# A convolution, attention and mixture-of-experts kernel: parts of the second convolution on ScalarE and GpSimd, fewer small copies, and VectorE's bursts cut into parts

## The chip, the cores and the metric

The kernel runs on one core of a Trainium2 chip. The core has TensorE (PE, matrix products), VectorE (DVE), ScalarE (ACT) and GpSimd (POOL), and SyncE (SP), whose queue here issues most DMAs. Each engine takes its own instructions in the order in which they stand in its queue. The metric is the device time of one launch in microseconds; a median over several launches is given.

## The reference

The input is 8 images of 56 x 56 positions with 256 channels, in float32. Two layers follow.

```python
# layer 0: 32 paths p, each 256 -> 4 -> 4 -> 256 channels, with batch norms
h = relu(bn1(x @ W1[p] + B1[p]))             # 1x1, to 4 channels
h = relu(bn2(conv3x3(h, W2[p]) + B2[p]))     # 3x3, 4 to 4 channels
h = relu(bn3(h @ W3[p] + B3[p]))             # 1x1, back to 256 channels
x = relu(sum_over_paths(h) + x)
# layer 1, on tokens t = x as (8, 3136, 256)
y = layernorm(t)
k = v = layernorm per head of 32 channels(y)       # std with n - 1
t = t + (y @ (k^T v / N) per head + y)
z = layernorm(t)
t = t + z + sum over the two best of 8 experts of weight * (gelu(z @ w1[e]) @ w2[e] + b2[e])
```

Each token goes to the two experts with the largest router logits; their weights are the two softmax values scaled to a sum of one.

## The kernel before

The 25,088 tokens are cut into 56 chunks of 448 (8 image rows), seven to an image. A chunk passes through a software pipeline of slots. In slot s the kernel does the third convolution of chunk s (`conv3_steps`), the first of chunk s+2 (`conv1_steps`), the second of chunk s+1 (`conv2_steps`), the head statistics of chunk s-1 (`end_steps`), the attention of chunk s-8 (`attn_steps`), the routing of one or two chunks whose attention is done (`route_steps`), and some tiles of the experts (`moe_steps`). After the 56th chunk's slot come slots with attention, routing and experts alone, and at the end experts alone; this is called the tail.

The order of work on PE, ACT and DVE is written out by hand (`tc.manual_schedule`, line 74). Each list of steps has a stretch of the slot (its low and high end as fractions) and each step a cost; `issue` (L1368) puts every step at the middle of its share of the stretch and issues all of a slot's steps in the order of these positions. Costs thus set places only. POOL and SP are not among the engines ordered by hand: the framework's planner places their instructions.

The parts that the change and the prediction's steps touch:

- Third convolution. For each of 32 steps of a chunk, `pair` (L577) makes two products c (L587); ACT turns the first into r (L592), and DVE adds the second to r (L595). Each product has a PSUM bank of seven (`ps_mm`); r has seven buffers. `sum_paths` (L601) sums four r at a time on PE (su, L608), a unit; there are eight units in a chunk. The sum of unit u stands after the pairs of the unit that follows have begun. After the fourth and the eighth unit DVE makes u (L615).
- Second convolution. After the three rows of taps (L297) ACT writes h2 (L306). The step `halves` (L309) splits it on DVE into hi (L314, rounded) and lo (L315, the rest), which sixteen DMAs on SP (L320) spread into hl, the operand of the next slot's third convolution.
- Head statistics. `means` (L665, a reduction of t and a scaling, both DVE), `center` (L679, POOL), `squares` (L687, ACT), `variances` (L695, eight DVE operations and then the square root as a power on POOL, L719), `inverse` (L723, DVE, which needs that power), `scale` (L735, POOL) and `products` (L742, PE).
- Attention. `attend` (L866) for four quarters: a product, an addition on DVE (L874), the copy of the router's part lg on ACT (L878, put off by one quarter), and token statistics on DVE (L881, L882); after the last the power rs2 on POOL (L885). `means` (L887) then makes nm on DVE, `normed` (L893) the normalised tokens in the payload pay on ACT, and `base` (L899) adds them to X on POOL and stores X.
- Routing. `logit`, `best` twice, `weights`, `ranks` and `rows` (L938 to L1028), nearly all DVE. `rows` writes into a token's payload row its two weights (L1019, L1020) and its number (L1021, from the constant ids) and the place of its row. `scatter` (L1030) then sends the rows by indirect DMAs on POOL into the regions of the experts.
- Experts. `take_rows` (L1220) and `take_weights` (L1231) load a tile of 256 rows (tile z, tag rows, four buffers) and its expert's weights w (four buffers) on SP. `tile_in` (L1239) turns the rows on PE, copies them on ACT (L1249), and copies the rows' weights g (L1252) and numbers index (L1256) on DVE. `tile_mid` (L1279) and `tile_out` (L1295) make the two layers; ACT scales by g into y (L1311); `tile_add` (L1316) adds y into the output by an indirect DMA on POOL (L1325).
- Setup. L487 to L494 split the second bias b2 into two halves, with buffers in the pool of constants, which lives through the kernel.

## Time and profile before

| | us |
|---|---|
| median of 3 runs (lowest, highest) | 3382.8 (3377.44, 3388.03) |
| the profiled execution | 3376.6 |
| its span, first to last instruction | 3374.9 |
| PE busy / DVE busy | 3001.6 / 2179.8 |
| ACT busy / POOL busy | 1895.8 / 1928.4 |
| mean granted PE clock | 0.951 of full speed |

How the views are read. The page's first part has an engine's busy time, its share of the span and its number of instructions (PEld is the loading of weights on PE). The busy time by stretch has, for each stretch of the span, its length and then PE, PEld, DVE, ACT and POOL (with instruction counts), the granted PE clock, the share of DMA busy time and GB/s. A tile's view gives the shortest, median and longest duration of each operation on it in ns, and below who waited for it, in us and times. A line of the order in time has the start and the length in us, engine, line, operation, output and inputs, shape and count, and in brackets how long the engine stood idle before it and what ended that.

### The profile page before, as it was taken

The numbers are of one execution on the slowest core, as the hardware profiler recorded it, in microseconds if no ns is written. First come the engines' busy times: TensorE is split into PE (matmuls) and PEld (weight loads), VectorE is DVE, ScalarE is ACT, GpSimd is POOL, SyncE is SP. The second block draws the span as 40 slices with busy tenths as digits, with TensorE's granted clock in tenths as the row PEclk, the third lists the DMA queues.
The fourth block names the chain that finished last, engine by engine and source line by source line (L and its number), as shares of the span: only waits on it lengthen the run. The fifth ranks groups of instructions, "written<-read, shape, count | busy, mean of one in ns | idle before, by whom it ended". The sixth has DMA issues, their size and how long they took to land. (4 is left out here: it accounts for less than half of the span.)

```text
span 3374.9 us, 55166 instructions
## 1 busy us (share of the span) xinstructions
PE 3001.6 (89%) x16677; PEld 1697.5 (50%) x16677; DVE 2179.8 (65%) x5762; ACT 1895.8 (56%) x3799; POOL 1928.4 (57%) x1386
## 2 busy tenths in 40 slices
PE   5888888888898999999999999899989987888698
PEld 2343433443444554555545555455444545676577
DVE  3666777777877777776776777776777774333200
ACT  2656555545565666566655666566656654443345
POOL 2222244444556566657565666746656657777677
PEclk7999989989999999999999999999999999988799
DMA  6432334445466676666666667567665756888797
GB/s 146 121 86 84 91 103 123 120 123 150 129 162 159 164 197 168 166 165 174 175 163 163 159 185 187 148 177 187 158 180 152 187 149 159 201 217 218 173 222 178
DMA packets 341481, 537.72 MB, mean 159 GB/s; under 512 B 59952, under 2 KB 251584, under 8 KB 341184
## 3 DMA queue, kind: packets, MB, share of 16 engines
q1 hardware_dynamic: 257088, 429.93, 43.8%
q0 software_dynamic: 81984, 103.45, 16.9%
q8 instruction: 134, 2.20, 0.3%
q14 instruction: 163, 1.34, 0.1%
q10 hardware_dynamic: 2112, 0.81, 0.1%
HBM read 248.01 MB, written 192.55 MB: 131 GB/s over the span
## 5 line engine op out<-in xcount | busy, mean ns | idle before, releaser
L595 DVE SCALAR_TENSOR_TENSOR r<-c,nb,r 128x448 f32<-128x448 f32 x1792 | 1127.3, 676 | 556.7 <-ACT r L592 482.8
L592 ACT ACTIVATE r<-c,b3t 128x448 f32<-128x448 f32 x1792 | 1033.2, 636 | 359.4 <-PE c L587 338.6
L1325 POOL DMA_INDIRECT out_dram<-y,index x420 | 662.8, 1578 | 356.3 <-ACT y L1311 243.7
L587 PE MATMUL c<-hl,W3hl 64*128 64x448 f32 x3584 | 708.4, 428 | 74.4 <-ACT r L592 37.7
L608 PE MATMUL su<-r,gather 128*32 128x448 f32 x3584 | 574.5, 568 | 64.9 <-DVE r L595 38.4
L1031 POOL DMA_INDIRECT regions<-pay,rrowi x448 | 433.1, 967 | 314.1 <-PE c L587 204.2
L587 PEld LDWEIGHTS c<-hl,W3hl 64*128 64x128 f32 x3584 | 341.9, 188 | 505.6 <-issue 227.1
L1287 PE MATMUL ph<-eT,w 128*128 128x256 f32 x1680 | 468.1, 410 | 55.7 <-DMA w<-Wd 23.8
L1307 PE MATMUL py<-w,hT 128*128 128x256 f32 x1680 | 435.6, 384 | 0.0
L1311 ACT ACTIVATE y<-py,g 128x256 f32<-128x256 f32 x420 | 196.7, 475 | 402.1 <-PE py L1307 303.1
L1287 PEld LDWEIGHTS ph<-eT,w 128*128 128x128 f32 x1680 | 306.9, 198 | 196.9 <-issue 101.8
L719 POOL TENSOR_TENSOR hsd<-hsd,half 112x36 f32<-112x36 f32 x56 | 351.7, 6280 | 78.4 <-DVE hsd L718 77.7
L1291 ACT ACTIVATE hT<-ph,w 128x256 f32<-128x256 f32 x420 | 198.1, 477 | 308.5 <-PE ph L1287 165.6
L1307 PEld LDWEIGHTS py<-w,hT 128*128 128x128 f32 x1680 | 293.9, 193 | 28.7
L681 POOL TENSOR_TENSOR norm<-t,hmean 112x512 f32<-112x512 f32 x112 | 120.2, 1130 | 322.1 <-PE c L587 175.0
L870 PE MATMUL at<-tab,tT 128*112 128x272 f32 x896 | 266.1, 421 | 11.9 <-ACT y L1311 6.8
L608 PEld LDWEIGHTS su<-r,gather 128*32 128x32 f32 x3584 | 104.2, 110 | 272.9 <-issue 135.5
L1303 PE MATMUL py<-b2hl,own 128*128 128x256 f32 x420 | 178.7, 425 | 22.4 <-ACT pay L894 8.1
L870 PEld LDWEIGHTS at<-tab,tT 128*112 128x112 f32 x896 | 149.4, 181 | 92.0 <-issue 17.3
L297 PE MATMUL c<-R,W2t 96*32 96x448 f32 x1344 | 180.1, 567 | 3.9 <-DMA R<-h 3.0
L894 ACT ACTIVATE pay<-X,nm,rs 112x256 f32<-112x256 f32 x224 | 134.9, 603 | 75.1 <-DVE nm L889 64.4
L976 POOL TENSOR_TENSOR rq<-ebase,rq 112x8 f32<-112x8 f32 (+1 forms) x32 | 52.9, 1654 | 197.0 <-DVE rq L975 197.0
(246 smaller groups left out, 3198.5 us busy)
## 6 DMA issues: line engine op xcount, KB each, us to landing
w<-Wd SPq DMA_DIRECT2D x210, 513.0 KB
rows<-regions SPq DMA_DIRECT2D x210, 259.0 KB
xi<-in_x_dram SPq DMA_DIRECT2D x56, 448.0 KB
hl<-hi SPq DMA_DIRECT2D x448, 56.0 KB
tTs<-u SPq DMA_DIRECT2D x56, 448.0 KB
ts<-t SPq DMA_DIRECT2D x56, 448.0 KB
tT<-tTs SPq DMA_DIRECT2D x56, 448.0 KB
X<-ts SPq DMA_DIRECT2D x56, 448.0 KB
```

What stands on the lines that cost most here:

```text
L587: product = nc.tensor.matmul(tiles[g][:, :CH], W3hl[rows, ab, cg, :], hl[rows, ab, :], start=True, stop=True)
L592: nc.scalar.activation(r, tiles[0][:, :CH], AF.Relu, bias=b3t[:, cg, 2 * ab : 2 * ab + 1])
L595: nc.vector.scalar_tensor_tensor(r, tiles[1][:, :CH], nb3[:, cg, 2 * ab + 1 : 2 * ab + 2], r, op0=ALU.max, op1=ALU.add,)
L608: nc.tensor.matmul(ps[32 * c4 : 32 * c4 + 32, :CH], gather, unit.pop((s, 4 * u + c4)), start=(ab == 0), stop=(ab == NQ - 1),)
L719: nc.gpsimd.tensor_tensor(sd, sd, half[:T, :].rearrange("q (k h) -> q k h", k=KT), ALU.pow)
L870: nc.tensor.matmul(ps, tT[:, f, k * T : (k + 1) * T], tables_of[b][:, f, :], start=(f == 0), stop=(f == NF - 1),)
L1031: ins = nc.gpsimd.indirect_dma_start(out=regions[n], out_offset=bass.IndirectOffsetOnAxis(ap=v["row_i"][:, (m - group[0]) * KT + k, n : n ...
L1287: nc.tensor.matmul(ps, w[:, f * C + hf * P : f * C + (hf + 1) * P], eT[:, f, :], start=(f == 0), stop=(f == NF - 1),)
L1291: nc.scalar.activation(hT[:, hf, :], ps, AF.Gelu, bias=w[:, 2 * NF * C + hf : 2 * NF * C + hf + 1])
L1307: nc.tensor.matmul(ps, hT[:, f, h * P : (h + 1) * P], w[:, (NF + f) * C : (NF + f + 1) * C], start=False, stop=(f == NF - 1),)
L1311: nc.scalar.activation(y[:, h, :], ps, AF.Identity, scale=g[:, h : h + 1])
L1325: ins = nc.gpsimd.indirect_dma_start(out=out_rows, out_offset=at, in_=y[:, h, :], in_offset=None, compute_op=ALU.add, **partial,).ins
```

## The change

- Second convolution: ACT makes both h2 and hi from the PSUM bank (the same activation twice); lo is made by POOL instead of DVE.
- Head statistics: a helper `in_parts` cuts a step into n parts of equal cost, each running to the next `yield`. `means` becomes three parts (two half reductions, then the scaling, now on ACT), with a cost of 0.8 instead of 0.6; `variances` five, `inverse` two.
- Attention: each quarter becomes two parts; the copy of lg and the token statistics stand in the second. A step `number` writes the tokens' numbers into the payload by an iota on POOL; the following `means` has half its cost.
- Routing: `logit`, `best`, `weights` two parts each, `rows` three. The weights are written straight into the payload, without a copy, and the numbers are no longer written there.
- Experts: g is a view of the row tile z and no copy; z has five buffers.
- Setup: the split of b2 moves ahead, with its two intermediate buffers in the setup pool; ids goes.

```diff
@@ -225,6 +225,19 @@
     nc.gpsimd.memset(h1[:, 1 : HW + 1, 0:1], 0.0)
     nc.gpsimd.memset(h1[:, 1 : HW + 1, HW + 1 : W58], 0.0)
 
+    def in_parts(cost, n, fn):
+
+        run = []
+
+        def part(k):
+            if not run:
+                run.append(fn())
+            for _ in run[0]:
+                if k < n - 1:
+                    return
+
+        return [(cost / n, lambda k=k: part(k)) for k in range(n)]
+
     def is_chunk(s):
         return 0 <= s < S
 
@@ -303,16 +316,16 @@
             if dy == 2:
                 del tapped[s]
                 h2 = split.tile([P, CH], F32, tag="h2", name=f"h2_{s}")
-                nc.scalar.activation(h2, ps[0][:, :CH], AF.Relu, bias=sh2, scale=sc2)
-                h2s[s] = h2
+                hi = split.tile([P, CH], F32R, tag="hi", name=f"hi_{s}")
+                for part in (h2, hi):
+                    nc.scalar.activation(part, ps[0][:, :CH], AF.Relu, bias=sh2, scale=sc2)
+                h2s[s] = (h2, hi)
 
         def halves():
 
-            h2 = h2s[s]
-            hi = split.tile([P, CH], F32R, tag="hi", name=f"hi_{s}")
+            h2, hi = h2s[s]
             lo = split.tile([P, CH], F32R, tag="lo", name=f"lo_{s}")
-            nc.vector.tensor_copy(hi, h2)
-            nc.vector.tensor_tensor(lo, h2, hi.bitcast(F32), ALU.subtract)
+            nc.gpsimd.tensor_tensor(lo, h2, hi.bitcast(F32), ALU.subtract)
             hl = hlp.tile([P, NQ, CH], F32R, tag="hl", name=f"hl_{s}")
             for ab in range(NQ):
                 for v, part in enumerate((hi, lo, hi, lo)):
@@ -415,6 +428,15 @@
         nc.vector.tensor_reduce(
             sumb[:, f, :], sub.rearrange("q a n -> q (a n)"), AX.X, ALU.add
         )
+
+    b2hl = const.tile([P, C], F32R, name="b2hl")
+    b2s = setup.tile([P, C], F32, name="b2s")
+    b2l = setup.tile([E, C], F32R, name="b2l")
+    nc.gpsimd.memset(b2s, 0.0)
+    nc.sync.dma_start(out=b2s[:E], in_=b2)
+    nc.vector.tensor_copy(b2hl, b2s)
+    nc.vector.tensor_tensor(b2l, b2s[:E], b2hl[:E].bitcast(F32), ALU.subtract)
+    nc.sync.dma_start(out=b2hl[E : 2 * E].bitcast(F32), in_=b2l.bitcast(F32))
     setup_pool.__exit__(None, None, None)
 
     spill = ctx.enter_context(
@@ -483,15 +505,6 @@
         tc.dram_tile([E * CAPR, ROW], F32, name=f"regions_{k}") for k in range(2)
     ]
     Wd = tc.dram_tile([E, P, WROW], F32, name="Wd")
-
-    b2hl = const.tile([P, C], F32R, name="b2hl")
-    b2s = const.tile([P, C], F32, name="b2s")
-    b2l = const.tile([E, C], F32R, name="b2l")
-    nc.gpsimd.memset(b2s, 0.0)
-    nc.sync.dma_start(out=b2s[:E], in_=b2)
-    nc.vector.tensor_copy(b2hl, b2s)
-    nc.vector.tensor_tensor(b2l, b2s[:E], b2hl[:E].bitcast(F32), ALU.subtract)
-    nc.sync.dma_start(out=b2hl[E : 2 * E].bitcast(F32), in_=b2l.bitcast(F32))
     pos_i = const.tile([P, 2], I32, name="pos_i")
     pos = const.tile([P, 2], F32, name="pos")
     nc.gpsimd.iota(pos_i, [[P, 2]], base=0, channel_multiplier=1)
@@ -503,8 +516,6 @@
     nc.vector.tensor_copy(row_code, row_i)
     nc.vector.tensor_scalar(row_code, row_code, -1.0, float(E), ALU.mult, ALU.add)
 
-    ids = const.tile([T, KT], I32, name="ids")
-    nc.gpsimd.iota(ids, [[T, KT]], base=0, channel_multiplier=1)
     def tiles_after(n):
 
         return max(0, (CH * n - E * (TR - 1)) // TR)
@@ -664,10 +675,14 @@
 
         def means():
             m = v["m"] = small([T, KT, NH], "hmean")
-            nc.vector.tensor_reduce(
-                m, v["t"].rearrange("q k (h c) -> q (k h) c", c=HC), AX.X, ALU.add
-            )
-            nc.vector.tensor_scalar_mul(m, m, 1.0 / HC)
+            for h in range(2):
+                nc.vector.tensor_reduce(
+                    m[:, 2 * h : 2 * h + 2],
+                    v["t"][:, 2 * h : 2 * h + 2].rearrange("q k (h c) -> q k h c", c=HC),
+                    AX.X, ALU.add,
+                )
+                yield
+            nc.scalar.mul(m, m, 1.0 / HC)
 
         def heads(t):
 
@@ -696,9 +711,13 @@
 
             sd = v["sd"] = small([T, KT, NH + 1], "hsd")
             ss = small([T, KT, NH], "hss")
-            nc.vector.tensor_reduce(
-                ss, v["sq"].rearrange("q k (h c) -> q (k h) c", c=HC), AX.X, ALU.add
-            )
+            for h in range(2):
+                nc.vector.tensor_reduce(
+                    ss[:, 2 * h : 2 * h + 2],
+                    v["sq"][:, 2 * h : 2 * h + 2].rearrange("q k (h c) -> q k h c", c=HC),
+                    AX.X, ALU.add,
+                )
+                yield
             m = v["m"]
             mu = small([T, KT], "hmu")
             dm = small([T, KT, NH], "hdm")
@@ -707,10 +726,12 @@
                 dm, mu[:, :, None].to_broadcast([T, KT, NH]), -1.0 / NH, m,
                 op0=ALU.mult, op1=ALU.add,
             )
+            yield
             nc.vector.tensor_mul(dm, dm, dm)
             nc.vector.scalar_tensor_tensor(
                 dm, dm, float(HC), ss, op0=ALU.mult, op1=ALU.add
             )
+            yield
             nc.vector.tensor_reduce(mu, dm, AX.X, ALU.add)
             nc.vector.tensor_scalar(
                 sd[:, :, NH], mu, 1.0 / C, LN_EPS, ALU.mult, ALU.add
@@ -729,6 +750,7 @@
                 op0=ALU.mult, op1=ALU.add,
             )
             nc.vector.reciprocal(inv, inv)
+            yield
             rs1s[s] = keep.tile([T, KT], F32, tag="rs1", name=f"rs1_{s}")
             nc.vector.reciprocal(rs1s[s], sd[:, :, NH])
 
@@ -755,8 +777,9 @@
                 nc.vector.tensor_add(kvs[b], kvs[b], ps)
 
         return [
-            (0.1, begin), (0.6, lambda: turn(0)), (0.6, lambda: turn(1)), (0.6, means),
-            (1.0, center), (0.6, squares), (1.8, variances), (0.8, inverse), (0.8, scale),
+            (0.1, begin), (0.6, lambda: turn(0)), (0.6, lambda: turn(1)),
+            *in_parts(0.8, 3, means), (1.0, center), (0.6, squares),
+            *in_parts(1.8, 5, variances), *in_parts(0.8, 2, inverse), (0.8, scale),
             (1.9, products),
         ]
 
@@ -861,7 +884,6 @@
         mv = stat.tile([T, KT, 2], F32, tag="mv", name=f"mv_{a}")
         rs2 = keep.tile([T, KT], F32, tag="rs2", name=f"rs2_{a}", bufs=4)
         nm = stat.tile([T, KT], F32, tag="nm", name=f"nm_{a}")
-        late = []
 
         def attend(k):
 
@@ -875,9 +897,8 @@
                 X[:, k, :], ps[:, :C], rs1[:, k : k + 1], X[:, k, :],
                 op0=ALU.mult, op1=ALU.add,
             )
-            late.append(lambda: nc.scalar.copy(lg[:, k, :], ps[:, C:]))
-            if k:
-                late.pop(0)()
+            yield
+            nc.scalar.copy(lg[:, k, :], ps[:, C:])
             nc.vector.bn_stats(st[:, k, :], X[:, k, :])
             nc.vector.bn_aggr(mv[:, k, :], st[:, k, :])
             if k == KT - 1:
@@ -885,9 +906,14 @@
                 nc.gpsimd.tensor_tensor(rs2, rs2, mhalf[:T, :KT], ALU.pow)
 
         def means():
-            late.pop(0)()
             nc.vector.scalar_tensor_tensor(
                 nm, mv[:, :, 0], -1.0, rs2, op0=ALU.mult, op1=ALU.mult
+            )
+
+        def number():
+
+            nc.gpsimd.iota(
+                pay[:, :, C + 2].bitcast(I32), [[T, KT]], base=a * CH, channel_multiplier=1
             )
 
         def normed(k):
@@ -908,8 +934,8 @@
             pays[a] = (pay, lg, rs1, rs2)
 
         return (
-            [(1.0, lambda k=k: attend(k)) for k in range(KT)]
-            + [(0.6, means)]
+            sum((in_parts(1.0, 2, lambda k=k: attend(k)) for k in range(KT)), [])
+            + [(0.3, number), (0.3, means)]
             + [(0.4, lambda k=k: normed(k)) for k in range(KT)]
             + [(0.6, base)]
         )
@@ -944,6 +970,7 @@
                     mine, raw[:, :, :E], rs1[:, :, None].to_broadcast([T, KT, E]), ALU.mult
                 )
                 nc.vector.tensor_add(mine, mine, raw[:, :, E:])
+                yield
 
         dsc = desc[:T, None, :].to_broadcast([T, K, E])
 
@@ -963,6 +990,7 @@
                 )
             nc.vector.tensor_reduce(mx, lg, AX.X, ALU.max)
             nc.vector.tensor_tensor(sel, lg, wide(mx), ALU.is_equal)
+            yield
             nc.vector.tensor_tensor(sel, sel, dsc, ALU.mult)
             nc.vector.tensor_reduce(at, sel, AX.X, ALU.max)
             nc.vector.tensor_tensor(sel, dsc, wide(at), ALU.is_equal)
@@ -974,6 +1002,7 @@
                 mine = q[:, n * KT : (n + 1) * KT]
                 nc.vector.tensor_mul(mine, mine, pays[m][3])
             nc.gpsimd.tensor_tensor(q, ebase[:T, :K], q, ALU.pow)
+            yield
             both = v["both"] = small([2, E], "rboth", BF16)
             nc.vector.tensor_copy(both, v["sel"])
 
@@ -1011,14 +1040,15 @@
         def rows():
             q2 = v["q"]
             q1 = small([], "rq1")
-            nc.vector.tensor_scalar_add(q1, q2, 1.0)
-            nc.vector.reciprocal(q1, q1)
+            nc.vector.scalar_tensor_tensor(
+                q1, q2, 1.0, half[:T, :K], op0=ALU.add, op1=ALU.max
+            )
             for n, m in enumerate(group):
                 pay = pays[m][0]
                 mine = slice(n * KT, (n + 1) * KT)
-                nc.vector.tensor_copy(pay[:, :, C], q1[:, mine])
-                nc.vector.tensor_mul(pay[:, :, C + 1], q2[:, mine], q1[:, mine])
-                nc.vector.tensor_scalar_add(pay[:, :, C + 2].bitcast(I32), ids, m * CH)
+                nc.vector.reciprocal(pay[:, :, C], q1[:, mine])
+                nc.vector.tensor_mul(pay[:, :, C + 1], q2[:, mine], pay[:, :, C])
+                yield
             row = small([2], "rrowf")
             row_i = v["row_i"] = stat.tile(
                 [T, 2 * KT, 2], I32, tag="rrowi", name=f"rrowi_{group[0]}"
@@ -1042,8 +1072,9 @@
                 del pays[m]
 
         return [
-            (0.5, logit), (0.5, lambda: best(0)), (0.5, lambda: best(1)), (0.5, weights),
-            (0.6, ranks), (0.5, rows),
+            *in_parts(0.5, 2, logit), *in_parts(0.5, 2, lambda: best(0)),
+            *in_parts(0.5, 2, lambda: best(1)), *in_parts(0.5, 2, weights),
+            (0.6, ranks), *in_parts(0.5, 3, rows),
         ], [
             [(0.5, lambda n=n, m=m, k=k: scatter(n, m, k)) for k in range(KT) for n in range(2)]
             for m in group
@@ -1208,7 +1239,7 @@
         return value
 
     def empty_rows(e):
-        pad = slots.tile([P, 2, ROW], F32, tag="rows", name=f"pad_{e}")
+        pad = slots.tile([P, 2, ROW], F32, tag="rows", name=f"pad_{e}", bufs=5)
         nc.gpsimd.memset(pad, 0.0)
         for k in range(2):
             ins = nc.sync.dma_start(
@@ -1219,7 +1250,7 @@
 
     def take_rows(i):
         row = entry(i, 0, E * CAPR - TR)
-        z = slots.tile([P, 2, ROW], F32, tag="rows", name=f"rows_{i}")
+        z = slots.tile([P, 2, ROW], F32, tag="rows", name=f"rows_{i}", bufs=5)
         region = regions[slot_of[i][2]]
         ins = nc.sync.dma_start(
             out=z, in_=region[bass.ds(row, TR), :].rearrange("(h p) c -> p h c", p=P)
@@ -1247,9 +1278,7 @@
                 )
         eT = work.tile([P, NF, TR], F32, tag="eT", name=f"eT_{i}")
         nc.scalar.copy(eT, tp)
-
-        g = slots.tile([P, 2], F32, tag="g", name=f"g_{i}")
-        nc.vector.tensor_copy(g, z[:, :, C + k])
+        g = z[:, :, C + k]
         index = slots.tile([P, 2], I32, tag="index", name=f"index_{i}", bufs=6)
         low = slot_of[i][3]
         if low is None:
```

## The prediction

> **What bounds the kernel now.** I read the page first, then stretches, then who waits for the slowest GpSimd operation, then single slots. The page gives the busy shares:

> ```profile
> PE 3001.6 (89%) x16677; PEld 1697.5 (50%) x16677; DVE 2179.8 (65%) x5762; ACT 1895.8 (56%) x3799; POOL 1928.4 (57%) x1386
> ```

> TensorE (PE) is the busiest, but unevenly. The busy time by stretch (slots before attention; slots with attention and no expert tiles yet; slots with all three; the tail):

> ```profile
> 98.00:366.00 268.00, 230.82 (x1317) 101.77 (x1317) 183.27 (x350) 159.09 (x289) 71.66 (x35) 0.98 0.32 92
> 366.00:833.00 467.00, 390.36 (x2152) 181.39 (x2153) 356.21 (x882) 254.79 (x493) 204.55 (x140) 0.91 0.41 119
> 833.00:2772.00 1939.00, 1826.16 (x10451) 979.64 (x10450) 1425.53 (x3680) 1190.28 (x2387) 1185.00 (x804) 0.98 0.64 168
> 2818.00:3375.00 557.00, 451.02 (x2264) 381.71 (x2262) 147.96 (x686) 234.48 (x526) 408.95 (x292) 0.91 0.81 199
> ```

> PE (third figure) is idle 37, 77, 113 and 106 us. From 833 us on it is at 94%, so what VectorE (DVE) saves there counts only where PE waits for DVE. The tile hsd shows one such place, GpSimd's (POOL) power at L719, 6.16 us long, behind which DVE stands at L727 and then PE at L608:

> ```profile
> L719 POOL TENSOR_TENSOR hsd<-hsd,half x56: 6124/6159/6738, 121.1 to 2866.2; 112x36 f32<-112x36 f32 x56
> ...
>   DVE hinv L727: 75.3, 47
>   PEld su L608: 42.1, 20
>   PE su L608: 19.9, 8
> ```

> An early slot in order of time (the slot begins at 290):

> ```profile
> 312.29 0.17 DVE L718 TENSOR_SCALAR hsd<-hss 112x32 f32<-112x32 f32 x1
> 312.54 6.12 POOL L719 TENSOR_TENSOR hsd<-hsd,half 112x36 f32<-112x36 f32 x1 [6.70 <-DVE hsd L718]
> 312.97 2.61 DVE L595 SCALAR_TENSOR_TENSOR r<-c,nb,r 128x448 f32<-128x448 f32 x4
> ...
> 318.70 0.19 DVE L727 SCALAR_TENSOR_TENSOR hinv<-hsd 112x32 f32<-112x32 f32 x1 [2.16 <-POOL hsd L719]
> ...
> 319.94 1.53 PE L608 MATMUL su<-r,gather 128*32 128x448 f32 x4 [2.24 <-DVE r L595]
> ```

> DVE works in order, so behind L727 stand the r additions (L595) that the sixth unit's sum (L608) needs; a 2.16 us wait costs PE 2.24 us. A slot with experts:

> ```profile
> 1489.59 6.63 POOL L719 TENSOR_TENSOR hsd<-hsd,half 112x36 f32<-112x36 f32 x1
> 1490.17 1.28 DVE L595 SCALAR_TENSOR_TENSOR r<-c,nb,r 128x448 f32<-128x448 f32 x2
> ...
> 1496.26 0.19 DVE L727 SCALAR_TENSOR_TENSOR hinv<-hsd 112x32 f32<-112x32 f32 x1 [0.99 <-POOL hsd L719]
> ...
> 1497.49 1.53 PE L608 MATMUL su<-r,gather 128*32 128x448 f32 x4 [0.53 <-issue]
> ```

> Taking, slot by slot, the time from the end of each r addition to the sum that reads it: in the sixth unit it is 0.1 us in 40 of 56 slots, so there the sum starts as soon as DVE is done. No other unit is so tight (third 29, eighth 27).

> [...]

> ```profile
> 1628.20 2.42 POOL L681 TENSOR_TENSOR norm<-t,hmean 112x512 f32<-112x512 f32 x2
> 1628.33 2.33 DVE L1019 COPY pay<-rq 112x4 f32<-112x4 f32 x1
> ```

> A copy that takes 0.16 us elsewhere lasts 2.33 us; but under the power at 1489.59 a DVE cast took its usual 0.38 us. [...] Here the wait ending at 1652.65 (2.17 us) is followed by a granted clock of 0.50 from 1652.7 to 1656.1[...]; such a window loses up to 1.7 us of PE work.

> **The change part by part.** The sums stand against the profiled execution, 3376.6 us (span 3374.9 and 1.7 around it); the median of the runs is 3382.8, 6.2 above, and I carry that over.

> *Variances in five parts, inverse in two.* A step sits at the middle of its share of the slot. Before, the chunk's steps cost 8.8 over 0.12–1.0: variances at 0.560, inverse at 0.690. After, they cost 9.0: the last variances part, which alone issues the power, at 0.640, inverse at 0.677. Between power and inverse DVE had the sum of unit 3 (0.68 us), four r additions (2.6), nm (0.15) and the halves (1.0); now two r additions and nm, 1.4 us, against 6.2 of power. So DVE will stand at hinv 4–5 us instead of about 1.6. Only the later end of the power counts. Early slot: ACT's r for pair 19 ends at 313.0, its addition at 313.7, the part's three small operations take 0.55, the power runs 314.4–320.5: hinv at 320.6 instead of 318.7, 1.9 later. Expert slot: pair 19 added by 1491.45, then 0.55, power to 1498.2: 2.0 later. The same reading for slots 1 to 55, less the slack that each sixth unit has, gives 86 us, 1.5 a slot (0 in the five slots where POOL started the power late anyway, 2.0–2.4 in the short ones). Behind hinv stand pairs 22 and 23, then PE's sum. In the stretches with PE at 94% it comes out nearly whole: I take 80 (30 if DVE, relieved, reaches the last part sooner or PE's other waits shrink; 115 if pair 19 is added as late as now).

> *Clock.* More waits of 2–4 us: one half-rate window in about five slots, 56/5 x 1.7 = +20 (0 to 60).

> *DVE's relief.* Gone: hi 22.4, lo 35.0, g 48.5, pay copies 40.6, numbers 24.4, hmean scaling 11.4: 182 us; L1014/L1015 (16.4) are replaced by about as much. Most lies under waits for ACT or beside a busy PE. On PE's path are the third unit's waits after rows and means: 2.8 us at 475.8, 568.5, 661.1 and 807.7. I count 5 such slots x 2.8, 12 later slots with plan or image steps x 2.0, 17 other routing slots x 1.0: −55 (−15, if they hide behind hinv, to −110, twice that).

> *ACT.* hi adds 56 x 0.73 (as L306), the hmean scaling 56 x 0.17 (as L878), which also waits in order for DVE's second half reduction. ACT is 61% busy; in the 18 slots before the experts the next r stands right behind: 18 x 0.3 = +5 (0 to 20).

> *lo on POOL.* L681 takes 1.05 us for 512 elements, so 448 take 0.92[...]. The time is hidden by POOL's idle 43%; its place is not. POOL's order and SP's are the planner's. lo becomes ready within about 1 us of the power. Ahead of it, it delays the power by up to 1.4; behind it, lo comes 6 us late, and the sixteen hl loads on SP (0.63 us each) stand behind, with R, rows and w loads after them. The first four are needed at the next slot, some 10 us away: +8 (0 to 150).

> *Row weights from the tile, five row buffers; numbers by iota; later lg copies; b2 in setup.* A row buffer is now held until y (L1311) of its tile, so the rows load on SP waits for y of three tiles before; the w load behind it already waits for py of that same tile (SP waits 345.8 us there). So it costs y's 0.5 us lag, covered by two tiles of lead; in the tail, where ACT stood 10–17 us behind nm, w would come late. iota 0.13 each (as L507). lg frees its bank half a step sooner. The three b2 operations only change place. Together +4 (−15 to +25).

> Sum: 80 + 20 − 55 + 5 + 8 + 4 = +62: 3438.6 for a profiled execution, 3445 median.

> **Rivals.** *Faster:* DVE's relief decides. For it: PE waits for DVE at unit 3 in 29 slots. It needs hinv's delay under 0.9 us a slot (about 50 us in all, what the relief gives); then relief −80, hinv +25, the rest +10: −45, 3338. Against it: the sixth unit's slack of 0.1. *Much slower:* lo is queued behind the power or waiting scatters, and PE starts slots waiting for hl: 2 us x 50 more, 3545. Against it: hl has some 10 us in hand. *Cancelled:* hinv's 80 and the clock's share shrink to the relief's size, 3383; the parts then change nothing that shows.

> **How the numbers follow.** Forecast 0.58, faster 0.21, much slower 0.12, cancelled 0.09. The range 3345–3530 takes all of the forecast's own (3395–3530) and cancelled, part of faster's upper half and of much slower's lower end. A measurement of this kernel tells about 0.3% (10 us) from no change: faster 0.21, same 0.09, slower 0.70.

> **What would show it.** Right: the wait of L727's successor for the power near 4–5 us in nearly all slots (some 200 us in all, from 75); PE waiting for r additions at the sixth unit about 2 us more; more slices with PEclk under 9; DVE busy near 2000. The relief: unit 3's 2.8 us gaps gone. lo behind the power: SP waiting long for lo at L320's successor, PE for hl at slot starts. Wrong: hinv's wait grown but PE's sixth-unit wait not, or main slots still near 46–53 us.

## The result and the profile after

| | before | after |
|---|---|---|
| median of four runs on one chip, us | 3385.41 | 3686.01 |
| ratio after/before, 95% interval | | 1.0893 (1.0862 to 1.0923) |
| span of the profiled execution, us | 3374.9 | 3686.5 |
| mean granted PE clock | 0.951 | 0.909 |

The changed kernel is 301 us slower. The forecast was 3445 us with a range up to 3530: the sign was right, the size was a fifth of what came. Line numbers in the changed kernel: r on ACT is L603 and on DVE L606, c L598, su L619, the power L740, hinv L748, lo L328, attention's power L906, nm L909, scale L759, kv L769.

Busy time by engine, first part of the page of the changed kernel:

```profile
PE 3133.3 (85%) x16677; PEld 1763.4 (48%) x16677; DVE 2158.6 (59%) x5408; ACT 1945.3 (53%) x3911; POOL 1995.0 (54%) x1497
```

PE runs the same 16,677 instructions and is busy 131.7 us longer (3133.3 − 3001.6). The span is 311.6 us longer, so the other 179.9 us is time in which PE does nothing. DVE, which the change was to relieve by some 180 us, is busy only 21 us less.

The same four stretches (early slots, attention without experts, all three, tail), with the columns of the table before:

```profile
103.00:404.00 301.00, 247.75 (x1318) 112.89 (x1318) 183.35 (x344) 163.96 (x302) 79.34 (x42) 0.90 0.29 82
404.00:909.00 505.00, 413.15 (x2149) 194.52 (x2149) 352.82 (x857) 260.85 (x511) 215.87 (x157) 0.87 0.39 112
909.00:3069.00 2160.00, 1918.42 (x10450) 1025.32 (x10450) 1422.56 (x3468) 1224.34 (x2461) 1226.30 (x876) 0.92 0.58 150
3124.00:3686.00 562.00, 450.18 (x2266) 378.00 (x2262) 134.66 (x581) 237.27 (x528) 411.33 (x299) 0.92 0.80 198
```

The tail is as before (562 against 557). The loss lies in the slots: 33 us in the early ones, 38 in the second stretch, 221 in the third. The granted clock (the figure after POOL) fell from 0.98 to 0.90, from 0.91 to 0.87 and from 0.98 to 0.92.

The tile hsd, with the duration of its operations in ns (shortest/median/longest) and who waited:

```profile
L740 POOL TENSOR_TENSOR hsd<-hsd,half x56: 6123/6160/6748, 127.8 to 3169.6; 112x36 f32<-112x36 f32 x56
L748 DVE SCALAR_TENSOR_TENSOR hinv<-hsd x56: 191/1102/1220, 133.9 to 3176.1; 112x32 f32<-112x32 f32 x56
...
  DVE hinv L748: 272.9, 56
```

The power lasts as long as before. DVE stands at hinv in all 56 slots, 272.9 us together (75.3 before), and hinv's own median is 1102 ns, where its mean was 191 before.

An early slot in order of time:

```profile
340.12 0.17 DVE L739 TENSOR_SCALAR hsd<-hss 112x32 f32<-112x32 f32 x1
340.37 6.12 POOL L740 TENSOR_TENSOR hsd<-hsd,half 112x36 f32<-112x36 f32 x1 [8.40 <-DVE hsd L739]
...
346.46 1.13 POOL L328 TENSOR_TENSOR lo<-h,hi 128x448 fp32r<-128x448 f32 x1
346.53 1.10 DVE L748 SCALAR_TENSOR_TENSOR hinv<-hsd 112x32 f32<-112x32 f32 x1 [4.25 <-POOL hsd L740]
...
347.97 2.42 DVE L606 SCALAR_TENSOR_TENSOR r<-c,nb,r 128x448 f32<-128x448 f32 x4
...
348.68 2.29 PE L619 MATMUL su<-r,gather 128*32 128x448 f32 x4 [5.00 <-DVE r L606]
```

This is the chain of the prediction (power, hinv, r, sixth unit's sum) with one addition: after DVE's wait of 4.25 us hinv itself takes 1.10 us, beside lo, which POOL starts at the same moment (with lo on DVE it takes 0.19 again, last series). PE stands 5.00 us where it stood 2.24. The r's behind hinv are what it stands for: ACT has made four of them by 343.60, DVE, which takes its instructions in order, adds them from 347.97, and the first of them ends as the sum begins. Two lines of the list of waits (waiter, what ended the wait: us in all, times, longest) give the sum over the kernel:

```profile
PE su L619 <- DVE r L606: 195.0, 56, 8.1
PE ph L1316 <- DVE r L606: 65.0, 25, 7.7
```

The first was 38.4 us before. Of the 195.0 us, 182.7 lie at the sixth unit's sum, where PE stood 50.6 us before, whatever ended the wait. The second is a wait for a PSUM bank: an expert product needs a bank that holds a c which DVE hasn't read yet. PE then stands there instead of at the sum.

How large the stops are can be worked out from the order of DVE's work in the two traces. Between the power's last input and hinv DVE was busy 294.4 us in all before (four r additions a slot, u, hi and lo) and 97.0 us after (two r additions): 197.4 less. The stops grew by as much, from 75.3 to 272.9.

### The profile page after: what moved, and what is told of

It is laid out like the page before. It is cut to its first block, busy times and chain, and to the rows that moved or that the text cites. A ratio compares the mean times of both kernels' runs of the same rounds, so it can differ in the third digit from the quotient of the medians.

```text
span 3686.5 us, 55060 instructions
## 1 busy us (share of the span) xinstructions
PE 3133.3 (85%) x16677; PEld 1763.4 (48%) x16677; DVE 2158.6 (59%) x5408; ACT 1945.3 (53%) x3911; POOL 1995.0 (54%) x1497
## 5 line engine op out<-in xcount | busy, mean ns | idle before, releaser
L606 DVE SCALAR_TENSOR_TENSOR r<-c,nb,r 128x448 f32<-128x448 f32 x1792 | 1129.3, 676 | 591.4 <-ACT r L603 567.0
L603 ACT ACTIVATE r<-c,b3t 128x448 f32<-128x448 f32 x1792 | 1028.2, 635 | 375.1 <-PE c L598 365.9
L598 PE MATMUL c<-hl,W3hl 64*128 64x448 f32 x3584 | 766.3, 440 | 82.2 <-ACT r L603 38.0
L619 PE MATMUL su<-r,gather 128*32 128x448 f32 x3584 | 618.9, 611 | 195.0 <-DVE r L606 195.0
L598 PEld LDWEIGHTS c<-hl,W3hl 64*128 64x128 f32 x3584 | 375.9, 195 | 563.6 <-issue 206.0
L1316 PE MATMUL ph<-eT,w 128*128 128x256 f32 x1680 | 499.3, 431 | 107.0 <-DVE r L606 65.0
L1316 PEld LDWEIGHTS ph<-eT,w 128*128 128x128 f32 x1680 | 322.8, 209 | 276.5 <-issue 89.5
L1340 ACT ACTIVATE y<-py,rows 128x256 f32<-128x256 f32 x420 | 197.0, 475 | 379.1 <-PE py L1336 321.1
L740 POOL TENSOR_TENSOR hsd<-hsd,half 112x36 f32<-112x36 f32 x56 | 348.2, 6218 | 78.3 <-DVE hsd L739 76.7
L619 PEld LDWEIGHTS su<-r,gather 128*32 128x32 f32 x3584 | 106.6, 113 | 404.4 <-DVE r L606 285.2
L892 PE MATMUL at<-tab,tT 128*112 128x272 f32 x896 | 253.0, 405 | 6.8 <-ACT y L1340 5.8
L896 DVE SCALAR_TENSOR_TENSOR X<-at,rs,X 112x256 f32<-112x256 f32 x224 | 107.2, 479 | 173.2 <-PE at L892 172.5
L748 DVE SCALAR_TENSOR_TENSOR hinv<-hsd 112x32 f32<-112x32 f32 x56 | 40.4, 721 | 272.9 <-POOL hsd L740 272.9
```

The lines of the kernel that those rows point to most:

```text
L598: product = nc.tensor.matmul(tiles[g][:, :CH], W3hl[rows, ab, cg, :], hl[rows, ab, :], start=True, stop=True)
L603: nc.scalar.activation(r, tiles[0][:, :CH], AF.Relu, bias=b3t[:, cg, 2 * ab : 2 * ab + 1])
L606: nc.vector.scalar_tensor_tensor(r, tiles[1][:, :CH], nb3[:, cg, 2 * ab + 1 : 2 * ab + 2], r, op0=ALU.max, op1=ALU.add,)
L619: nc.tensor.matmul(ps[32 * c4 : 32 * c4 + 32, :CH], gather, unit.pop((s, 4 * u + c4)), start=(ab == 0), stop=(ab == NQ - 1),)
L740: nc.gpsimd.tensor_tensor(sd, sd, half[:T, :].rearrange("q (k h) -> q k h", k=KT), ALU.pow)
L892: nc.tensor.matmul(ps, tT[:, f, k * T : (k + 1) * T], tables_of[b][:, f, :], start=(f == 0), stop=(f == NF - 1),)
```

## The experiments

The first theory: the split of the variances moves the power back, DVE stops at hinv, PE stops behind it and loses its clock as well. Rivals: lo's place on POOL, and the rest of the change. Each difference below is to the median of the kernel before in the same series (3375.7, 3385.6, 3384.9, 3381.6 and 3379.1 us).

### First series: the split and lo

Whole steps again:

```diff
-            *in_parts(1.8, 5, variances), *in_parts(0.8, 2, inverse), (0.8, scale),
+            *in_parts(1.8, 1, variances), *in_parts(0.8, 1, inverse), (0.8, scale),
```

> The changed kernel with the variances as one step again (cost 1.8) and the inverse as one step (0.8); everything else of the change stays. Theory (the split sets the power back by about 8% of a slot, DVE then stands at hinv for 4 to 5 us, PE stands for r, and the clock drops for it): hinv's wait falls from 4.9 to about 1.5 us a slot, the half-rate time of the slots falls back to about the 180 us of the kernel before, and the time is 3340 to 3420 us. Rival one (lo behind the power on GpSimd is the cost): lo stays where it is, the time stays above 3550. Rival two (the rows' buffers, numbers and weights, or the spreading of attention and means): the time stays above 3600.

The kernel before with the split alone (the reverse edit there):

> The kernel before with nothing but the variances in five parts and the inverse in two, as the changed kernel has them; hi and lo stay on VectorE. Theory: this alone brings most of the loss, 3560 to 3690 us, with a wait of 4 to 5 us at hinv in nearly every slot. Rival one (lo on GpSimd): below 3450, since lo isn't on GpSimd here. Rival two (the other parts): 3380 to 3430.

lo on DVE in the changed kernel:

```diff
-            nc.gpsimd.tensor_tensor(lo, h2, hi.bitcast(F32), ALU.subtract)
+            nc.vector.tensor_tensor(lo, h2, hi.bitcast(F32), ALU.subtract)
```

> The changed kernel with lo made by VectorE again, hi still by ScalarE. hinv's instruction should last 0.19 us again in place of 0.72, which is up to 0.9 us off the stop of every slot; VectorE gets some 0.9 us a slot of work back. Theory: the later power is the larger part and stays, so the time is 3580 to 3670 us. Rival one: most of the loss goes, 3380 to 3450. Rival two: no change within 15 us.

Still split, but with room between the power and hinv:

```diff
-            *in_parts(1.8, 5, variances), *in_parts(0.8, 2, inverse), (0.8, scale),
+            *in_parts(1.0, 5, variances), (0.8, lambda: None), *in_parts(0.8, 2, inverse), (0.8, scale),
```

> The changed kernel, still split in five and two parts, but the five parts of the variances have a cost of 1.0 in place of 1.8 together, and an empty step of 0.8 stands between them and the inverse: the power is issued some 5% of a slot sooner, hinv stays at its place, no step after it moves. Theory: it is the distance from the power to hinv that counts, so hinv's wait falls to about 1.5 us a slot or less, and the time is 3360 to 3450 us. If instead it is the splitting as such, or lo, or the rows' part, the time stays above 3600.

| | median, us | ratio to before (95%) | stops at hinv, us |
|---|---|---|---|
| split undone | 3581.4 | 1.061 (1.060 to 1.063) | 177.3 |
| split alone | 3725.7 | 1.103 (1.101 to 1.105) | 281.4 |
| lo on DVE | 3624.8 | 1.074 (1.072 to 1.075) | 238.8 |
| room for the power | 3560.1 | 1.055 (1.052 to 1.058) | 172.8 |

The split alone loses more than the whole change, 350 us, 36 above the end of its expectation. Part of that isn't in the changed kernel: lo, here on DVE and behind hinv, runs beside POOL's scale and takes 2.25 us in the mean in place of 0.63 (126.1 us in all, 35.0 before); in all DVE is busy 2242.4 us, 62.6 more than before. Undoing the split gives back only 95, and two expectations (3340 to 3420, 3360 to 3450) were missed by over 100 us. The stops at hinv tell part of why: with the steps whole they are still 177 us and not 75. In the kernel before, hi, lo and u (0.40, 0.63 and 0.68 us on DVE) stood between the power and hinv; here hi and lo have left DVE, and u stands ahead of the power, since by the costs the dearer `means` moves the whole variances some 1% of a slot back. DVE arrives at hinv earlier, while the power is as late as ever. lo on DVE again was inside its expectation, 51 us back (300.6 less 249.2).

### Second series: is the stop the cause?

hinv further behind the power (it stays behind the same r additions, and the power is issued two r's sooner):

```diff
-            *in_parts(1.8, 5, variances), *in_parts(0.8, 2, inverse), (0.8, scale),
-            (1.9, products),
+            *in_parts(0.6, 5, variances), (1.7, lambda: None), *in_parts(0.4, 2, inverse), (0.8, scale),
+            (1.7, products),
```

> The changed kernel with costs of 0.6 for the variances (still five parts), an empty step of 1.7, 0.4 for the inverse (two parts) and 1.7 for the products in place of 1.8, 0.8 and 1.9: hinv comes some 4 us of a slot further behind the power than in the changed kernel's order. All the work and VectorE's relief stay. Theory as it stands after the first runs (the loss follows VectorE's stop at hinv, 1.6 to 1.9 us of time for each us of stop summed over the slots, whichever edit brought it): hinv's stops fall under 75 us in all and the time is 3330 to 3420 us. Rival (the stop is only a symptom, another part of the change costs): the stops go and the time stays above 3500.

The kernel before with the move of hi and lo alone:

> The kernel before with hi by ScalarE and lo by GpSimd and nothing else; the variances and the inverse are whole. Theory: VectorE loses 1.0 us of work between the power and hinv and 1.4 us of ScalarE's work comes ahead of the same r's, so hinv's stops grow from 75 to some 130 to 180 us and the time to 3450 to 3570 us: the relief of VectorE is spent on waiting. Rival (a relief of VectorE helps as long as the power isn't moved): 3320 to 3380 us.

The changed kernel with whole steps and idle work on DVE:

```diff
             nc.gpsimd.tensor_tensor(lo, h2, hi.bitcast(F32), ALU.subtract)
+            for _ in range(3):
+                top = split.tile([P, 1], F32, tag="top", name=f"top_{s}_{_}", bufs=1)
+                nc.vector.tensor_reduce(top, h2, AX.X, ALU.max)
```

> The changed kernel with the variances and the inverse whole, as in the first run of this study (3581 us), and in addition three idle reductions of h2 to 128x1 on VectorE where lo is made, about 1.8 us a slot between the power and hinv; their results are not used. Theory: VectorE is given more work and the kernel still does not get slower, 3480 to 3590 us, because the stop at hinv shrinks by what the idle work takes (177 us in all to about 80). Rival (VectorE's work is the bound, the stop is not): 3640 to 3700 us, 1.1 us to 1.8 us a slot more.

The changed kernel with idle matmuls in PE's stop:

```diff
+    FILL = 20
...
         pace[:] = [product.ins]
+        if step == 25:
+            for _ in range(FILL):
+                nc.tensor.matmul(
+                    tiles[1][:, CH:512], ident, ident[:, : 512 - CH], start=True, stop=True
+                )
```

> The changed kernel with twenty idle matmuls of TensorE a slot (128x64, into columns of a PSUM bank that nobody reads) behind the c matmuls of step 25, just ahead of the sixth unit's sum, where TensorE stands for r. Theory that part of the loss is TensorE's clock, which drops after the stops: the granted clock of the main slots rises, TensorE's busy time without the idle matmuls falls by 40 to 130 us, and the time is 3560 to 3680 us in spite of 4 us more of matmuls a slot. Rival (the clock doesn't matter beside the stops): TensorE's other work takes as long as before and the time is 3690 to 3800 us.

| | median, us | ratio to before (95%) | stops at hinv, us |
|---|---|---|---|
| hinv further behind the power | 3547.2 | 1.047 (1.042 to 1.052) | 16.8 |
| hi and lo alone | 3448.1 | 1.017 (1.013 to 1.022) | 99.3 |
| idle work on DVE | 3630.8 | 1.072 (1.067 to 1.078) | 88.8 |
| idle matmuls | 3649.1 | 1.077 (1.071 to 1.082) | 272.5 |

*hinv further behind the power.* The stop went and the time stayed at 3547. The list of waits and the order of time of this kernel show what came in its place:

```profile
DVE nm L909 <- POOL rs L906: 217.8, 55, 21.6
...
DVE hinv L748 <- POOL hsd L740: 16.8, 8, 2.9
```

```profile
1623.77 6.16 POOL L740 TENSOR_TENSOR hsd<-hsd,half 112x36 f32<-112x36 f32 x1 [1.97 <-DVE hsd L739]
1629.91 1.00 POOL L906 TENSOR_TENSOR rs<-rs,mhalf 112x4 f32<-112x4 f32 x1
1630.95 0.16 DVE L909 SCALAR_TENSOR_TENSOR nm<-mv,rs 112x4 f32<-112x4 f32 x1 [1.64 <-POOL rs L906]
```

With the variances' cost at 0.6 the long power is issued ahead of attention's short one, which then waits out its 6 us on POOL; DVE stops at nm instead of hinv (77.3 us there in the changed kernel), and ACT's pay waits for nm. The stop had only moved, so this run doesn't decide between theory and rival.

*Idle work.* Here the theory fell. The stops at hinv shrank by 88.5 us (177.3 to 88.8) and the time did not stay: against the kernel before it rose by 39 us, from +206 to +245, to a place between the two expectations. The sum of the stops thus doesn't set the time. My reading is that a DVE that stands and a DVE that does useless work hold up the r's behind it alike; the idle reductions take 100.0 us, so some 11 us of them come on top, and the rest of the 39 isn't explained.

*hi and lo alone* lost 62 us, just under the expected 3450 to 3570, with stops of 99 and not of 130 to 180 us. So hi and lo make 24 of the 102 us by which the stops of the kernel with whole steps exceed those before. DVE's busy time didn't fall either: 2179.0 us against 2179.8, for other operations take longer (hinv 24.9 us, g 20.6, nm 14.9). The reason given for the loss, the stops, was wrong in the main, as the last series shows.

*Idle matmuls.* First part of the page of this kernel, and the group of the idle matmuls (engine, shapes, count | busy us, mean ns):

```profile
PE 3297.2 (91%) x18917; PEld 2000.7 (55%) x18917; DVE 2165.0 (59%) x5408; ACT 1941.7 (53%) x3911; POOL 1996.1 (55%) x1497
```

```profile
L606 PE MATMUL c<-ident 128*128 128x64 f32 x2240 | 287.6, 292 | 0.0
```

PE got 287.6 us of extra matmuls and the kernel became 37 us faster (300.6 less 263.5 over before). The idle matmuls overlap the others by some 9 us; without them PE is busy 3018.6 us in this trace, 115 less than in the changed kernel and little more than before the change (3001.6). The mean clock is 0.947 again. This shows the second half of the chain: some 115 of the 131.7 us by which PE's busy time grew are the clock, lost to the stops, and they come back if PE is kept at work during them, though hinv's stops (272.5) are what they were.

### Third series: both powers in order

```diff
-            *in_parts(1.8, 5, variances), *in_parts(0.8, 2, inverse), (0.8, scale),
-            (1.9, products),
+            *in_parts(1.3, 5, variances), (1.6, lambda: None), *in_parts(0.4, 2, inverse), (0.7, scale),
+            (0.5, lambda: None),
+            (0.7, products),
```

> The changed kernel with the power behind attention's power on GpSimd (variances 1.3 in five parts) and hinv far behind it (an empty step of 1.6, inverse 0.4, scale 0.7, an empty step of 0.5, products 0.7). In the run with hinv late (3547 us) the two powers had changed places, and VectorE stood at nm for 218 us in place of hinv. Theory (each us of stop on VectorE, at hinv or nm, costs 1 to 1.7 us): hinv's and nm's stops together fall under 120 us, and the time is 3380 to 3470 us. Rival (something else in the change costs some 150 us whatever these stops are): 3500 to 3560 us.

The same with attention's quarters whole:

```diff
+        late = []
...
-            yield
-            nc.scalar.copy(lg[:, k, :], ps[:, C:])
+            late.append(lambda: nc.scalar.copy(lg[:, k, :], ps[:, C:]))
+            if k:
+                late.pop(0)()
...
+            late.pop(0)()
...
-            sum((in_parts(1.0, 2, lambda k=k: attend(k)) for k in range(KT)), [])
+            [(1.0, lambda k=k: attend(k)) for k in range(KT)]
```

> The same as the run with both powers in order, with attention's four steps whole again and lg's copy deferred by one, as in the kernel before. In all runs that have attention's steps in halves, VectorE waits 140 to 178 us for attention's matmuls at X; in those that have them whole, 49 to 66 us. If that wait costs, the time falls by 50 to 150 us against the run with both powers in order; if it is time in which VectorE had nothing else to do, by less than 20 us.

That edit alone in the changed kernel:

> The changed kernel with attention's four steps whole again and lg's copy deferred, nothing else. If the wait at X costs: 3540 to 3640 us. If not: 3660 to 3700 us.

The kernel before, hinv a little later:

> The kernel before with an empty step of 0.4 between the variances and the inverse and the products' cost 1.5 in place of 1.9: hinv comes some 2 us a slot later, the power stays where it is. hinv's stops (75 us in the kernel before) fall under 25 us. Theory: the time falls by 50 to 100 us, to 3275 to 3330 us. Rival (the stops of the kernel before are covered): 3360 to 3390 us.

| | median, us | ratio to before (95%) |
|---|---|---|
| both powers in order | 3432.1 | 1.013 (1.010 to 1.017) |
| and attention whole | 3394.9 | 1.003 (1.001 to 1.004) |
| attention whole alone | 3612.6 | 1.067 (1.064 to 1.070) |
| before, hinv a little later | 3390.0 | 1.002 (1.001 to 1.003) |

Places alone, with every other part of the change kept, take 253 of the 301 us away (300.6 less 47.2). The list of waits of the kernel with both powers in order:

```profile
DVE nm L910 <- POOL rs L907: 105.3, 15, 18.2
...
PE kv L769 <- POOL norm L759: 45.1, 42, 3.1
...
DVE hinv L748 <- POOL hsd L740: 11.0, 9, 5.8
```

The edit keeps the power behind pair 17, as in the kernel before, and puts hinv behind pair 25, four r's later. Both stops of DVE are small together (116.3 us, under the expected 120), and there is a next one: PE waits 45 us at kv for scale, which now comes late in the slot. Attention's quarters in halves, for which my sum had no term, cost 37 us here, less than the 50 to 150 expected and more than the 20 of no effect, and 73 us in the changed kernel (300.6 less 227.7). The last run is no evidence on stops: with an empty step of 0.4 hinv stands between the same r's on DVE as before.

### Fourth and fifth series: the rest of the loss

Scale and hinv two r's sooner (1.1 ahead of the inverse, 1.0 behind scale), attention whole:

> The run with both powers in order and attention whole, with half of the first empty step moved behind scale (1.1 ahead of hinv, 1.0 behind it): hinv and scale come two r's sooner, so that TensorE no longer stands for scale at kv (37 us there before). Theory (what is left of the loss is that wait): 3340 to 3375 us. Rival (the work that VectorE is relieved of was hidden anyway): 3380 to 3400 us.

The same with hi and lo on DVE, as L314 and L315 were:

> The same with hi and lo made by VectorE again, as in the kernel before. If the relief of VectorE by hi and lo is worth something once no stop takes it back, this is slower than the run before it by 20 to 60 us; if that work is hidden, the two agree within 15 us.

The kernel before with nothing but new places:

```diff
-            (1.0, center), (0.6, squares), (1.8, variances), (0.8, inverse), (0.8, scale),
-            (1.9, products),
+            (1.0, center), (0.6, squares), (1.8, variances), (1.0, lambda: None), (0.8, inverse), (0.7, scale),
+            (0.3, lambda: None), (0.7, products),
```

> The kernel before with an empty step of 1.0 ahead of the inverse, so that hinv comes four r's later on VectorE (in the first try, with 0.4, VectorE's order stayed as it was), scale at 0.7, an empty step of 0.3, the products at 0.7. The 75 us of stops at hinv go. If each of them costs as in the changed kernel: 3280 to 3350 us. If they are covered in the kernel before: 3370 to 3395 us.

The kernel of the second of these runs, with hi on ACT, lo on DVE:

> The run with the kv wait taken out and hi and lo by VectorE (3331 us), with hi by a second activation of ScalarE again; lo stays on VectorE. If ScalarE's 0.72 us more ahead of the r's are what hi and lo off VectorE cost (53 us in all), this is 3360 to 3385 us; if lo's place on GpSimd is, 3320 to 3340 us.

And with hi on DVE, lo on POOL:

> The same kernel with lo by GpSimd instead and hi by VectorE's copy. If lo on GpSimd is the cost (VectorE's hinv beside it lasts 1.1 in place of 0.19 us, and the GpSimd work behind lo comes 1.1 us later): 3360 to 3385 us; if ScalarE's second activation is: 3320 to 3340 us.

The kernel before with hinv two r's later:

```diff
-            (1.0, center), (0.6, squares), (1.8, variances), (0.8, inverse), (0.8, scale),
-            (1.9, products),
+            (1.0, center), (0.6, squares), (1.8, variances), (0.6, lambda: None), (0.8, inverse), (0.7, scale),
+            (0.7, lambda: None), (0.7, products),
```

> The kernel before with hinv two r's later on VectorE instead of four (empty step 0.6; scale 0.7, an empty step of 0.7, products 0.7), so that TensorE's wait for scale at kv, 29 us with four, goes as well: 3300 to 3335 us; 3336 us or more if that wait was covered.

| | median, us | less than before by | ratio (95%) |
|---|---|---|---|
| hi ACT, lo POOL | 3383.9 | −2 | 1.0005 (0.999 to 1.002) |
| hi DVE, lo DVE | 3331.0 | 51 | 0.985 (0.982 to 0.987) |
| hi ACT, lo DVE | 3318.8 | 60 | 0.983 (0.980 to 0.986) |
| hi DVE, lo POOL | 3394.7 | −16 | 1.005 (1.003 to 1.007) |
| before, hinv four r's later | 3335.8 | 46 | 0.986 (0.983 to 0.989) |
| before, hinv two r's later | 3308.9 | 70 | 0.981 (0.978 to 0.984) |

*The kv wait.* PE's idle time there fell from 36.7 to 13.5 us, and the stops at hinv, now two r's nearer to the power, rose from 11.7 to 51.0. The net gain is 8 us (10.1 less 2.3 over before), hardly clear of the noise; the rival's 3380 to 3400 was right and not the theory's 3340 to 3375. *hi and lo* were the surprise: I expected their return to DVE to cost 20 to 60 us or nothing, and it gained 53. One at a time, lo's place makes all of it: 63 us with hi on ACT, 66 with hi on DVE. hi on ACT costs nothing in either pair: with lo on DVE it is 10 us faster, by intervals that overlap (0.985 and 0.983), and with lo on POOL 13 us, by intervals that don't (1.0005 and 1.005). It is lo on POOL that costs, not ACT's second activation.

What lo does there is seen in part. hinv with lo on POOL and with lo on DVE, both with hi on ACT (group: busy us, mean ns | idle before):

```profile
L748 DVE SCALAR_TENSOR_TENSOR hinv<-hsd 112x32 f32<-112x32 f32 x56 | 52.3, 934 | 51.0 <-POOL hsd L740 51.0
```

```profile
L748 DVE SCALAR_TENSOR_TENSOR hinv<-hsd 112x32 f32<-112x32 f32 x56 | 10.6, 189 | 44.5 <-POOL hsd L740 44.3
```

That is 42 us of DVE's time. But with hi on DVE hinv is stretched by only 11.5 us in all, and lo costs as much. A slot of that kernel, POOL in order of time:

```profile
1541.96 6.12 POOL L740 TENSOR_TENSOR hsd<-hsd,half 112x36 f32<-112x36 f32 x1 [1.29 <-DVE hsd L739]
...
1551.86 1.74 POOL L328 TENSOR_TENSOR lo<-h,hi 128x448 fp32r<-128x448 f32 x1
...
1556.62 2.07 POOL L759 TENSOR_TENSOR norm<-norm,hinv 112x512 f32<-112x512 f32 x2
```

lo stands between the power and scale, so scale and kv come later. PE's waits at kv, of this kernel and then of the one with both on DVE:

```profile
PE kv L769 <- POOL norm L759: 21.1, 31, 1.5
```

```profile
PE kv L769 <- POOL norm L759: 8.8, 19, 0.8
```

Of the 66.4 us between these two profiles (spans of 3393.2 and 3326.8), 23.2 are PE's busy time (3011.8 and 2988.6) and 43.2 its idle time. The waits of PE that grew are 12.3 at kv and 38.1 for r's of DVE (16.4 at c, 15.8 at su, 5.9 at py); others shrank a little. Which instruction of POOL or DVE makes each of those r's late isn't separated, so it is shown that lo's place on POOL costs, and only in part how.

*The kernel before with new places alone* has the lowest median of all, 3308.9 us, inside the expected 3300 to 3335, and the stops that it had at hinv were not covered: 75.3 us of stops became 23.2 and the time fell by 70. PE's part in it:

```profile
PE 2985.9 (90%) x16677; PEld 1692.4 (51%) x16677; DVE 2173.5 (66%) x5762; ACT 1897.2 (57%) x3799; POOL 1926.5 (58%) x1386
```

DVE is busy 2173.5 us here and 2105.9 in the changed kernel with repaired places and lo on DVE (3318.8); the second is not faster. The 68 us less show no gain. The two differ in more than DVE's work, though (hinv's stops are 44.3 us in the second and 23.2 in the first), so what the relief is worth by itself isn't separated. With four r's in place of two the gain is 46: PE waits 29.2 us for scale at kv, against 4.3.

## Why the prediction was wrong

Of the signs that were to show the forecast right, the stop of 4 to 5 us in all slots and the longer waits at the sixth unit came; DVE busy near 2000 us did not (2158.6). The sign of the change follows from the first term. *Much slower*, 3545, stood nearest to the measured time, but by chance, for PE didn't start its slots waiting for hl. By the steps of the sum:

- *Variances in five parts, inverse in two, +80: undersized; this step failed first.* Its mechanism held in every link (later power, stop at hinv in all slots, sixth unit late). I wrote "DVE will stand at hinv 4–5 us", which was right (4.9 a slot), but let only the later end of the power count, 1.9 to 2.0 us, and charged 1.5 after slack. In the traces, over slots 1 to 55, the power ends 8.9 us after ACT's r for pair 19 in the mean, and 5.5 before: 3.3 later (2.5 in the median). The part's last operation ends on DVE 1.9 us after that r in the mean where I took 1.25, and POOL starts 0.75 us after it where I took 0.15. hinv beside lo adds 0.5 us a slot. So PE's idle time at the sixth unit's sum grew by 132.1 us (from 50.6 to 182.7), and there are 65.0 at expert products for a bank, a place that the sum didn't have: 197 against 80. In the changed kernel undoing the split gives 95 us and the repair of places 253. The parts don't add: several of them close the same gap between the power and hinv.
- *Clock, +20: the term most out of size.* The count, an estimate of mine, was one half-rate window in about five slots. By the records of the granted clock, the 38 slots with all three kinds of work had 18 stretches at half rate before and 59 after, 88.7 and 348.2 us in all: a stretch lasts 5.9 us on average, and more than one comes in a slot. PE's same instructions took 131.7 us more, and with idle matmuls 115 of that came back. I had both the number and the length too small, from one slot with a stop of 2 us. The stretches in these records are multiples of 3.41 us, all but the last one of each trace. Cutting both traces into such windows and taking those at full rate: where PE was busy under 40% of one, half rate followed in all 29 cases before and all 44 after; where it was busy over 80%, in 0 of 746 and 3 of 716. A stop of just over 2 us inside one window (60% of 3.41 us is 2.05) puts it among the first.
- *DVE's relief, −55: the waits that it was to remove were not there.* That the third unit's sum starts right behind DVE in 29 slots I took for a wait in each. PE's idle time at that sum is 13.6 us in all before, in five slots, and 10.0 after (1.0 with repaired places and hi on ACT, lo on DVE). So about 13 us could be gained there. Nor were the 182 us all work. The copy of the weights into pay took 40.6 us: 24 of 56 took 0.73 to 2.88 us (35.5 us in all), all beside GpSimd's `center` (L681), as the one that I showed did; 16 others beside it took 0.16. Taking such copies away didn't take the delays away: g went, 48.5 us, but the copy of the numbers, unchanged in the source, took 52 us more (the two lines: before, then after). 25 of its 180 took over 1 us there, 61.5 us together, all beside long GpSimd operations; with repaired places it takes 34.6 again:

```profile
L1256 DVE COPY index<-rows 128x2 int32<-128x2 int32 x180 | 35.8, 199 | 55.0 <-DMA out_dram<-y,index 40.4 <-issue 14.6
L1285 DVE COPY index<-rows 128x2 int32<-128x2 int32 x180 | 88.0, 489 | 111.6 <-DMA out_dram<-y,index 50.2 <-DMA rows<-regions 45.2 <-issue 16.2
```

- *lo on POOL, +8 (0 to 150): 63 to 66 measured with the places repaired (51 in the changed kernel), and by another way.* I had weighed a late hl, as did the rival *Much slower*; in the changed kernel c waited once for hl, for 12.4 us. As far as shown, lo's cost is its place on POOL, beside hinv and ahead of scale. In the changed kernel 32 of the 56 hinv's run beside lo and take 1.12 us in the mean, the 24 others 0.19. Not every pair does this: under the power DVE's lo took 0.63 us before (47 of 56 ran under it), as it did beside other work; beside POOL's scale, in the kernel with the split alone, it took 2.25. What sets the one kind of pair apart from the other was not shown. I had looked at such a delay for a copy of the kernel before and not for the pair that the change brings together.
- *ACT, +5: no cost shows.* With hi on ACT the time is lower by 10 and 13 us (3318.8 and 3331.0, 3383.9 and 3394.7).
- *Row weights, iota, lg, b2, +4:* SP's waits ahead of the experts' loads moved from py (345.8 us) to y (359.3 us) as written. These parts were not tried alone; with the places repaired and lo on DVE, all that remains of the change costs nothing that shows (3318.8 against 3308.9, with intervals that overlap).
- *Missing:* attention's quarters in halves, 37 to 73 us. I read them as a change of lg's bank alone. DVE waits for attention's products at X 172.5 us in the changed kernel and 56.9 before. Why halves cost that much was not taken further than these two numbers and stays open.

From the changed kernel to 3318.8 us the shown steps are: places 253, attention 37, kv 8, lo 63; together 361, which is the 301 of the loss and 60 beyond. These are steps in this order; in another order each could come out otherwise.

## What to carry to other kernels

Before relieving an engine that works in order, or moving its work, look for the long operation elsewhere that this work was covering. Here VectorE's work between the power and hinv fell by 197.4 us, and its stops rose by 197.6. lo, placed right behind the power, came on top: hinv beside it took 1.10 us in place of 0.19. Before booking an operation's time as relief, see whether it is work or a wait for another engine, and whether TensorE waits for it at all. Charge a stop of a few microseconds on the way to TensorE twice, once for its length and once for the clock: of 311.6 us, 131.7 are longer busy time of the same matmuls. Look at places first: moving hinv two r's back, with scale behind it, gave 70 us in a kernel where a change meant to take some 180 us of work off VectorE lost 301.
